# Two gated cross-attention layers on one core: maxima of the first attention read from PSUM, products of ones ahead of TensorE's work, moments by pairs, a new order

## The chip, the cores and the metric

The kernel runs on one core of a Trainium2 chip. A core has a matrix engine (TensorE, PE in the profile, with its weight loads as PEld), three engines for element-wise work (VectorE or DVE, ScalarE or ACT, GpSimd or POOL), and queues that start transfers (here SyncE, SP, and ACT). Each engine works through its own instructions in order and waits for others by semaphores. On-chip memory is SBUF; PE writes its results to PSUM, eight banks of 2 KB in each of 128 partitions, from where DVE or ACT fetch them.

The metric is device time in microseconds, the median of several runs. The profile is one execution, whose span runs from its first to its last instruction.

## The reference

The input `x` has 2 x 1024 rows of 256 features; the context has 2 x 77 rows. Two layers follow each other. Each adds a gated cross-attention (16 heads of 16 features, 77 keys) and a gated feed-forward part. In the first layer the feed-forward part has quantized weights (three levels) and activations (8 bits) and a GELU; in the second it is one expert with a ReLU and a layer norm at its end, since the routing weight is one for expert 0 and zero for the others. The second attention adds a bias from the distances.

```python
x = x + jnp.tanh(g_xattn[0]) * _L0_xattn_ref(_layernorm(x), ctx, ctx_weights...)
x = x + jnp.tanh(g_ffn[0]) * _L0_ffn_ref(_layernorm(x), L0_ffn_w1, L0_ffn_w2)
x = x + jnp.tanh(g_xattn[1]) * _L1_xattn_ref(_layernorm(x), ctx, ctx, distances, ...)
x = x + jnp.tanh(g_ffn[1]) * _L1_ffn_ref(_layernorm(x), ...)
# attention: softmax(q k^T / 4 [- log(distances + 1e-9) * |scaling|]) v, then the output weights
# first FFN: quant(gelu(quant(h) @ quant(w1).T)) @ quant(w2).T
# second FFN: relu(h @ w1 + b1) @ w2 + b2, layer norm of h plus that, times gamma, plus beta
```

All arithmetic is in fp32, apart from the quantized products, whose integers are held in bf16.

## The kernel before

The 2048 rows are 16 tiles of 128 rows, in four groups of four tiles (`GROUPS`). Each group goes through four stages: attention of layer one (`attention(0, g)`), quantized feed-forward (`bit_ffn`), attention of layer two (`attention(1, g)`), expert (`expert_ffn`). Groups don't depend on each other, so stages of different groups overlap.

**Order.** The kernel doesn't issue its work as it is written. Every step (one or a few instructions on one engine) is recorded in a `Plan` with a cost, the tiles that it reads and writes, and for some steps two engines to choose from. `Plan.order` then goes through a list schedule: on each engine the step that can begin first, ties decided by the number that the table `WEIGHTS` (line 52) has for the step. Buffers are given out in the same pass. The steps are issued in the order of their planned begin, and the tile framework adds the semaphores that this order needs. So a step's cost, or its weight, changes where it stands on its engine and which buffer it gets. Transfers are one exception: they are planned in the order in which they are written, and those that ACT starts are issued first of all.

**The beginning.** `fetch` (line 464) starts the transfers: the first group's rows tile by tile on SP, the weights of the first attention on ACT's queue, then the rest. POOL makes constants, one of them `ones` (line 560). PE's first work is `center` (line 765), which takes the mean of the query weights out of them, and the transposes of the first rows (line 663).

**Attention.** For a group, PE transposes the rows (663) and makes the queries (803). Then, for each half of the heads and each pair of tiles, `softmax_pair` runs:

- PE makes the scores of both tiles (827), 16 products into `sc`, four PSUM banks, of which there is one set;
- in the first layer ACT copies each tile's scores to SBUF (the helper's line 427, `probs<-sc`); in the second DVE adds the distance bias on the way (866);
- DVE takes the maximum per row and head from the copy (875), POOL subtracts it (880), ACT takes the exponential (889), DVE sums (897) and takes reciprocals (902), POOL multiplies (906).

`values` then has PE transpose the probabilities (925), ACT copy them (427, `pT<-b`), and PE multiply them by the values (938). The output weights (959) and the gated residual (967) end the stage, with the moments of the new rows.

**Moments.** `stats` (line 587) adds two steps for each tile of 128 rows: `bn_stats` (589) and `bn_aggr` (590). POOL makes the reciprocal root from them (609, 610).

**Feed-forward parts.** `bit_ffn` rounds (1079) and transposes (1093) rows, multiplies by the quantized weights (1132), takes GELU on ACT (1140), takes the maximum of the hidden rows on DVE (1056), rounds, transposes and multiplies again (1156), and adds the residual (1164). `expert_ffn` has two large products, 1192 and 1211. Two tiles share one PSUM bank for the result of 1211; DVE adds it (1227), takes moments (589), and two more steps (1239, 1247) lead to the store. For the last pair of the last group these steps are taken tile by tile.

Of the kernel before, what the change touches and what calls it, by code (L numbers as in the profile page):

```python
# [9 lines left out]
F32 = mybir.dt.float32  # L10
# [6 lines left out]
P = 128  # L17
# [31 lines left out]
LEAVE = 2  # L49

# [3 lines left out]
1245 1326 1308 1686 1626 1573 1612 1393 1342 1295 1643 1706 1629 1687 1420 1685 1486 1673 1711  # L54
1665 1126 1335 1606 1580 433 1173 843 1317 1350 761 989 905 630 1053 674 1167 919 1052 748 1329
710 1713 1547 1634 1720 1705 1597 1557 1717 1684 1455 1518 1562 1497 1633 1664 1651 1649 1417 1691
1504 1642 1698 1690 1696 1718 534 1552 1513 1106 1033 483 1659 1000 1670 718 1407 512 904 491 600
408 699 479 467 1668 1716 1457 1641 1596 1478 1621 1611 1639 1645 1628 1631 1671 1540 1590 1658
1662 1657 1677 1694 1707 1703 1689 1701 1640 1465 1680 1697 1661 1679 1427 1499 1714 1708 1636
1530 1704 1719 1377 1463 1374 1591 1700 1688 1683 1675 1494 1551 1702 1674 1647 1667 1715 1709  # L60
1517 1489 1579 1601 1444 1695 1462 1655 1318 1362 1178 1110 1346 1402 1156 1524 1570 1652 1627
1678 1425 1219 1587 1338 1269 1554 1365 1262 1413 1239 1537 1484 1446 1356 1321 1210 1360 1692
1663 1440 1630 1712 1710 1660 1646 1605 1517 1584 1268 484 885 1297 1035 1699 1625 1672 1608 1682
1693 1592 1621 1635 1410 1560 1530 1345 1488 1514 1614 1411 1526 1449 1404 1432 1649 1525 1533
1603 1472 1604 1599 1624 1576 1543 1516 1581 1560 1582 1366 1452 1399 1506 1615 1588 1281 1403
1653 1632 1472 1654 1456 1487 1249 1522 1527 1572 1236 1306 1438 1290 1666 1624 1173 1272 640 966
1565 271 1166 1072 1567 1151 959 740 1331 1091 1291 1264 1333 1267 1030 916 1182 1138 990 928 1256
983 1012 1120 829 762 1081 961 1235 974 1027 1032 723 677 1034 1499 861 1064 934 883 1261 399 1164
1011 889 1086 1062 1093 893 1154 560 1313 1325 827 1580 584 790 836 738 947 1163 869 1010 1423
1075 1250 1483 786 932 975 1108 845 615 903 1044 633 473 1337 409 1081 1349 840 1043 1401 1372 656  # L70
477 613 924 763 367 324 827 579 750 821 958 665 811 550 606 566 607 524 320 511 297 359 559 362
537 925 833 560 587 463 556 317 745 913 835 1299 1080 891 1016 986 1141 1098 1065 788 1037 777
1327 1104 969 519 1300 912 800 722 705 720 1203 901 799 1289 1253 1085 1111 900 1099 1121 1118 703
852 899 749 505 478 699 775 1041 1005 1090 789 887 908 1134 1185 772 711 724 957 727 315 901 772
796 848 1206 653 993 822 819 690 669 512 670 636 725 1014 975 1132 1102 1130 609 646 644 567 718
756 1201 563 647 948 710 629 627 648 592 1040 808 898 697 582 795 596 500 888 1189 558 520 1336
991 960 1116 856 846 530 818 741 759 976 434 1242 1333 967 1107 915 1055 517 931 576 278 328 319
355 516 394 639 835 558 186 210 241 257 372 295 253 458 684 544 894 444 679 1363 816 1379 1036
1022 1315 920 1419 1109 1538 678 246 759 412 410 358 419 407 366 600 746 726 342 588 594 488 801
216 228 194 312 963 733 487 1026 1183 862 1285 1232 1442 1301 1045 1193 1127 1347 831 1091 912 687  # L80
1424 1528 1529 868 850 512 708 345 752 742 548 635 844 896 851 1257 1135 1149 1171 1110 1051 896
334 341 1271 331 1009 231 301 157 265 343 313 823 855 681 910 369 249 218 266 287 457 510 565 707
619 651 436 154 298 435 572 404 381 153 196 167 161 410 1470 1123 1192 1316 1368 1361 1493 1324
1512 1284 1443 1379 1439 1322 1441 1263 1332 1276 1364 1389 1412 1577 1507 1481 1502 1535 1349
1331 1542 1369 1294 1428 1386 1548 1640 1503 1361 1638 1617 1588 1610 1421 1424 1622 1552 1595
1532 1589 1637 1405 1280 1506 1521 993 1385 1541 1619 1656 1174 1397 1360 1454 1354 1175 1574 1436
1561 1490 1112 1388 1409 1382 1429 1426 1177 1371 1213 1307 826 949 1610 1343 1344 1390 1509 1280
1294 1291 1351 1292 1312 1505 1435 1544 1461 1474 1304 1566 1165 1023 1476 1480 1193 1133 1214
1100 1380 1512 1272 1209 1401 1605 1539 1437 1448 1514 1451 1341 1464 1598 1585 1588 1555 1352
1613 1495 1644 1569 1618 1623 1586 1571 1632 1681 1512 1358 1669 1542 1231 1433 1377 1600 1279  # L90
1357 1536 1534 1607 1620 1568 1048 1278 1314 948 960 1223 1104 678 460 999 874 973 689 955 980
1013 719 822 773 847 1014 1048 1159 1348 367 625 706 474 753 1265 846 655 546 936 858 878 1067 866
555 705 1002 686 764 774 730 613 872 914 780 832 867 506 820 466 323 682 693 915 702 1293 815 1099
768 701 797 770 763 1069 1025 1378 1408 1018 1160 1079 876 950 1339 694 665 346 1063 1387 875 700
691 630 954 789 494 779 661 842 221 422 265 686 414 208 427 193 183 309 264 364 440 368 344 765
585 476 404 537 632 304 644 299 692 535 593 453 438 1508 1247 1447 1520 578 650 1477 1222 1305
1356 1074 1117 326 574 1088 769 380 349 445 397 470 538 574 413 695 582 657 542 557 700 825 496
763 860 623 384 549 879 1113 749 1084 1317 1248 964 917 1221 1185 946 1096 1078 1319 1174 1434 908
1399 951 962 1336 1095 1122 762 995 1283 1479 1468 1249 1147 1398 1000 1434 971 1265 1146 1196
1205 1260 1391 1252 1416 1353 1328 608 787 732 922 1016 942 853 1169 998 1075 1065 1323 1202 732  # L100
1460 1194 386 671 575 622 431 482 501 639 426 388 666 822 399 935 871 672 972 566 238 302 497 305
944 721 918 1144 660 1125 1222 1078 1084 791 247 376 926 739 1243 1517 1212 377 573 729 966 515
743 1021 1266 748 1001 985 714 1038 509 371 895 1162 873 717 751 1482 1054 1212 1286 1101 758 881
754 480 529 307 336 400 470 373 234 262 411 636 1153 1046 784 889 1317 711 782 620 715 325 232 418
624 552 979 1047 690 934 951 803 812 444 766 771 932 966 838 405 884 825 1168 451 878 806 1187
1181 1334 1032 1082 1396 737 1223 1020 1114 1232 713 1208 1140 976 1004 1066 1187 886 1149 1150
540 610 1240 1207 1496 1374 1377 1504 1511 1515 1362 1313 1027 1320 1223 1255 1542 1546 1545 1415
1474 1475 1273 1501 1007 1458 864 870 1075 1145 1296 1105 1228 1218 1217 1211 1192 1156 1259 1191
1087 890 1195 1037 1381 1301 1081 1172 851 1011 1140 1109 793 982 930 1198 1163 1395 1559 1523
1383 1225 1045 1025 1142 1265 1246 1028 1008 997 1077 1137 809 1311 1161 1244 1231 923 929 996 968  # L110
1510 1270 1274 1024 1364 1070 1309 1277 1282 1425 1531 1450 1253 1650 1676 1609 1575 1584 1445
1466 1558 1578 1553 1469 1302 1563 1375 1220 1430 1492 1453 1401 1330 1288 1224 1216 938 1550 1556
1648 1616 1583 1361 1402 1473 1498 1418 1301 1400 1396 1128 1068 1094 988 654 795 554 472 465 1452
779 595 801 849 1062 1066 1205 939 852 1031 1594 1188 1190 1157 1485 1593 1491 1139 747 1148 645
683 401 1029 1179 1061 909 767 350 718 406 1070 673 1067 577 424 643 956 1219 1226 896 694 449
1076 508 811 795 792 1215 911 603 901 810 790 882 329 980 1195 698 1071 692 765 1124 1076 1049 705
1195 1089 561 611 798 931 957 946 953 945 646 958 902 471 518 689 614 230 364 592 545 649 704 375
739 867 443 589 929 786 1166 663 1234 860 1273 834 668 600 709 428 679 972 778 937 1279 1230 1256
1312 1039 1413 696 1306 933 1186 940 992 570 280 318 300 225 786 528 454 490 201 261 308 486 378
365 330 289 316 310 237 486 396 459 539 242 338 139 1177 1282 924 450 197 415 442 127 244 169 314  # L120
269 430 450 449 599 417 779 532 471 755 239 531 177 117 158 120 267 191 254 227 281 500 498 637
568 655 525 675 794 527 1305 598 573 623 856 988 536 449 512 479 676 535 583 920 716 829 465 503
452 514 949 275 332 626 256 590 638 374 245 143 721 1015 187 135 147 390 347 124 121 182 205 160
200 185 229 141 156 163 110 98 62 20 27 91 76 72 151 89 125 162 108 155 150 172 105 142 175 152 17
# [101 lines left out]
class Plan:  # L226
# [45 lines left out]
    def order(self, weight):  # L272
# [13 lines left out]
        while len(done) < len(self.steps):  # L286
            best = None
            for e, waiting in ready.items():
                cand = []
                for s, w, at in waiting:  # L290
# [8 lines left out]
                    for t in s.tiles:  # L299
                        if t in given:  # L300
                            continue
# [1082 lines left out]
```

## Time and profile before

| | |
|---|---|
| median of 3 runs | 372.38 us (371.84 to 373.26) |
| the profiled execution | 373.1 us |
| its span | 371.4 us |
| mean granted clock of TensorE | 0.973 |
| busy: PE, DVE, ACT, POOL | 338.6, 272.3, 238.7, 235.3 us |
| weight loads of PE (beside its products) | 214.7 us |
| subtractions and multiplications on POOL (880, 906) | 128 of 1.25 and 1.27 us |
| maxima and sums on DVE (875, 897) | 128 of 0.78 and 0.77 us |
| copies of scores on ACT (427, `probs<-sc`) | 32 of 0.69 us |

Durations of single instructions include the time in which the engine fills and drains, which overlaps with the next instruction. Where instructions stand back to back, the distance from start to start is the time that one more of them costs: 0.70 us for a maximum, 0.71 for a sum, 1.2 for a step on POOL. In the timeline and the chain, merged rows such as "x2" show this. "Idle before" in brackets names what ended the wait. Busy shares of the whole span mix stages that have different limits; the table by stretches keeps them apart.

### The profile page before, as it was taken

The page shows a single profiled execution, that of the slowest core. Times are in us where ns is not written, and L with a number is a line of the kernel's source. Part 1 is how long each engine was busy: PE and PEld are TensorE (multiplying, and loading weights), DVE is VectorE, ACT ScalarE, POOL GpSimd, SP SyncE. Part 2 cuts the span into 40 slices and gives each one's busy share as a digit, 9 for nine tenths or more (in the row PEclk, how much of TensorE's full clock was granted, in tenths as well). Part 3 has the DMA queues.
Part 4 walks back from the last instruction along what each step waited for, and adds up shares of the span by engine and source line. Part 5 has one row for each costly group of instructions (what it writes and reads, how often), then busy time and mean ns, then how long its engine had stood idle before and what let it go on. Part 6 is the DMA issues. An engine that isn't in the chain of part 4 may idle for free.

```text
span 371.4 us, 5881 instructions
## 1 busy us (share of the span) xinstructions
PE 338.6 (91%) x2148; PEld 214.7 (58%) x2156; DVE 272.3 (73%) x570; ACT 238.7 (64%) x395; POOL 235.3 (63%) x265
## 2 busy tenths in 40 slices
PE   5959899889978989899999999999999999999993
PEld 3535346466554755674474467675488546685582
DVE  3598778899999999999999986397325896074034
ACT  2597879899999897967778472727541386431400
POOL 5399799998995052599989976019213688144012
PEclk9996969998999999999999999999999999999998
DMA  8972002003010000000000000000000100000001
GB/s 236 354 207 41 5 22 92 2 6 109 3 14 3 3 2 0 2 2 2 0 3 0 2 0 2 29 2 0 28 2 22 35 2 1 3 0 29 28 2 57
DMA packets 18150, 12.51 MB, mean 34 GB/s; under 512 B 8647, under 2 KB 17608, under 8 KB 18120
## 3 DMA queue, kind: packets, MB, share of 16 engines
q1 hardware_dynamic: 17300, 11.34, 10.4%
q10 hardware_dynamic: 816, 0.79, 0.6%
q8 instruction: 17, 0.28, 0.3%
q14 instruction: 17, 0.11, 0.1%
HBM read 9.71 MB, written 2.10 MB: 32 GB/s over the span
## 4 chain that ended last, share of the span: by engine, by line
PE 50%; DVE 25%; ACT 10%; POOL 9%; issue 3%; DMA 1%; POOLq 0%; ACTq 0%; DVEq 0%
PE b L1211 14%; PE b L1192 12%; DVE mx L875 5%; POOL probs L880 5%; PE b L925 5%; PE b L938 5%; DVE den L897 4%; DVE probs L866 3%; DVE st L589 3%; PE sc L827 3%; PE b L803 3%; POOL probs L906 3%; DVE x L967 2%; ACT pT L427 2%; DVE top_h L1056 2%
## 5 line engine op out<-in xcount | busy, mean ns | idle before, releaser
L880 POOL TENSOR_TENSOR probs<-probs,mx 128x616 f32<-128x616 f32 x64 | 78.7, 1248 | 14.2 <-DVE mx L875 11.4
L906 POOL TENSOR_TENSOR probs<-probs,den 128x616 f32<-128x616 f32 x64 | 79.7, 1266 | 6.4 <-DVE den L902 4.1
L925 PE MATMUL b<-ident,probs 128*128 128x128 f32 (+1 forms) x320 | 49.4, 286 | 11.8 <-ACT pT L427 4.2
L1211 PE MATMUL b<-staged,hT 128*128 128x256 f32 x256 | 58.6, 381 | 0.6 <-DVE xn L1227 0.6
L1192 PE MATMUL b<-xnT,staged 128*128 128x512 f32 x128 | 57.0, 596 | 0.0
L925 PEld LDWEIGHTS b<-ident,probs 128*128 128x128 f32 (+1 forms) x320 | 36.6, 142 | 31.8 <-POOL probs L906 11.2
L875 DVE TENSOR_REDUCE mx<-probs 128x8 f32<-128x616 f32 x64 | 48.7, 784 | 8.1 <-ACT probs L427 7.3
L897 DVE TENSOR_REDUCE den<-probs 128x8 f32<-128x616 f32 x64 | 48.7, 772 | 7.2 <-ACT probs L889 7.2
L427 ACT ACTIVATE pT<-b 128x512 f32<-128x512 f32 (+1 forms) x80 | 44.4, 601 | 13.6 <-PE b L925 13.4
L1211 PEld LDWEIGHTS b<-staged,hT 128*128 128x128 f32 x256 | 47.5, 190 | 8.4 <-issue 1.5
L609 POOL TENSOR_SCALAR rstd<-mv 128x4 f32<-128x4 f32 (+2 forms) x25 | 7.6, 305 | 65.3 <-DVE mv L590 65.2
L427 ACT ACTIVATE hT<-b,eb_sb 128x512 f32<-128x512 f32 x32 | 21.7, 684 | 27.3 <-PE b L1192 21.5
L1192 PEld LDWEIGHTS b<-xnT,staged 128*128 128x128 f32 x128 | 23.5, 190 | 26.5 <-issue 25.1
L803 PE MATMUL b<-xnT,wq_sb 128*128 128x512 f32 x64 | 35.3, 660 | 0.3 <-ACT xnT L427 0.3
L633 ACT ACTIVATE xn<-x,shift,rstd 128x256 f32<-128x256 f32 x48 | 25.8, 595 | 13.1 <-DVE x L1247 8.5
L938 PE MATMUL b<-pT,vbd 128*32 128x512 f32 (+1 forms) x256 | 33.3, 627 | 0.4 <-ACT pT L427 0.4
L959 PE MATMUL b<-wo_sb,OT 128*128 128x256 f32 x128 | 30.4, 383 | 0.6 <-ACT OT L427 0.5
L589 DVE BATCH_NORM_STATS2 st<-x 128x6 f32<-128x256 f32 x64 | 25.8, 416 | 5.5 <-DMA x<-in_x_dram 4.5
L1227 DVE TENSOR_TENSOR xn<-b,xn 128x512 f32<-128x512 f32 (+1 forms) x9 | 5.7, 632 | 30.8 <-PE b L1211 30.8
L827 PE MATMUL sc<-kbd,qT 32*128 32x154 f32 x512 | 27.6, 325 | 0.6 <-ACT probs L427 0.4
L827 PEld LDWEIGHTS sc<-kbd,qT 32*128 32x128 f32 x512 | 19.4, 189 | 14.0 <-issue 3.4
L959 PEld LDWEIGHTS b<-wo_sb,OT 128*128 128x128 f32 x128 | 23.5, 190 | 5.5 <-ACT OT L427 1.2
(102 smaller groups left out, 541.1 us busy)
## 6 DMA issues: line engine op xcount, KB each, us to landing
staged<-in_ew_dram SPq DMA_DIRECT2D x2, 1024.0 KB
out_dram<-x SPq DMA_DIRECT2D x7, 256.0 KB
x<-in_x_dram SPq DMA_DIRECT2D x6, 256.0 KB
staged<-in_fw1T_dram SPq DMA_DIRECT2D x1, 1024.0 KB
staged<-in_fw2T_dram SPq DMA_DIRECT2D x1, 1024.0 KB
dbias<-in_dist_dram SPq DMA_DIRECT2D x1, 616.0 KB
x<-in_x_dram SPq DMA_DIRECT2D x4, 128.0 KB
wo_sb<-in_woT_dram SPq DMA_DIRECT2D x2, 256.0 KB
```

The costliest lines, as they stand in the source:

```text
L427: nc.scalar.activation(out(), src(), AF.Relu if relu else AF.Copy if bias is None else AF.Identity, bias=0.0 if bias is None else bias(), ...
L803: lambda h=h, k=k, pq=pq: nc.tensor.matmul(pq.ap, wq_sb.ap[:, k, h * P : (h + 1) * P], xnT.ap[:, k, :], start=(k == 0), stop=(k == KT - 1),),
L827: nc.tensor.matmul(sc.ap[:, q, j * QK : j * QK + QK], qT.ap[rows, h, at : at + P], kbd.ap[rows, h, b].rearrange("p h s -> p (h s)"), start ...
L875: lambda j, n: nc.vector.tensor_reduce(each(mx, j, n), heads(j, n), AX.X, ALU.max),
L880: lambda e, j, n: e.tensor_tensor(heads(j, n), heads(j, n), bc(each(mx, j, n), 2, SK), ALU.subtract),
L897: lambda j, n: nc.vector.tensor_reduce(each(den, j, n), heads(j, n), AX.X, ALU.add),
L906: lambda e, j, n: e.tensor_tensor(heads(j, n), heads(j, n), bc(each(den, j, n), 2, SK), ALU.mult),
L925: lambda j=j, c=c, m=m, tr=tr: nc.tensor.transpose(tr.ap[:m, j, :], prs[j // 2].ap[:, j % 2, c * P : c * P + m], ident.ap),
L938: nc.tensor.matmul(po.ap[32 * q : 32 * q + 32, :], vbd.ap[: CH[c], b, h, s, :], pTs[c].ap[: CH[c], :], start=(i < 4), stop=(i >= 4),)
L959: nc.tensor.matmul(pp.ap[:, j % 2, :], OT.ap[:, k, j * P : (j + 1) * P], wo_sb.ap[:, k, :], start=(k == 0), stop=(k == KT - 1),)
L1192: lambda f=f, k=k, ph=ph: nc.tensor.matmul(ph.ap, ew1_sb.ap[:, k, f * P : (f + 1) * P], xnT.ap[:, k, :], start=(k == 0), stop=(k == KT - 1),),
L1211: lambda j=j, f=f, pp=pp: nc.tensor.matmul(pp.ap[:, j % 2, :], hT[f].ap[:, j * P : (j + 1) * P], ew2_sb.ap[:, f, :], start=(f == 0), stop= ...
```

## The change

Five things change.

1. In the first layer the maximum (875) reads the scores in PSUM instead of the copy in SBUF. The copy stays, and the subtraction still needs both. The reduction keeps its order of elements in both layers.
2. `WARM` = 14 products of `ones` by `ones` into an unused PSUM tile are the first step of PE. `ones` is now made first.
3. `stats` takes one or two tiles in one step: both `bn_stats`, then both `bn_aggr`. Pairs are used after attention, after the expert, and for the rows of the later groups; single tiles for the first group's rows, after `bit_ffn` and for the last pair.
4. The last pair of the last group gets a PSUM bank for each tile.
5. The planner has new costs (transfers, copies, maxima, residuals, moments), keeps a step from beginning before the buffer of its tile is free, and has a new table of weights. The order on every engine is new. The first group's rows and weights are written in another sequence, which changes their place in the plan and not on their queues.

The number of instructions is almost the same: PE has 14 products more, ACT loads its tables eleven times instead of nine, one addition of a bias goes from DVE to POOL. In the new order the first layer's third group comes ahead of its second, and the expert of the first group begins ahead of the second attention of the second group, which it followed before.

```diff
+WARM = 14
 WEIGHTS = tuple(
...
                     for t in s.tiles:
                         if t in given:
+                            begin = max(begin, born[t])
                             continue
...
-                given[t] = min(slots[key])[1]
+                born[t], given[t] = min(slots[key])
...
-    def fetch(eng, t, src, cols=None):
+    def fetch(eng, t, src, cols=None, cost=None):
...
-            max(0.47, size / 0.28),
+            cost or max(0.47, size / 0.3),
...
+    fetch_x0(0, 1.6)
+    wq0_sb = fetched_w(nc.scalar, "wq0_sb", wqT0, None, 0.6)
+    fetch_x0(1, 0.5)
+    fetch_x0(2, 1.1)
+    wk0_sb = fetched_w(nc.scalar, "wk0_sb", wkT0, None, 0.6)
+    fetch_x0(3, 0.7)
...
+    warm = lazy(ps_b, [P, P], F32, "b", 4)
+
+    def warm_up():
+        for _ in range(WARM):
+            nc.tensor.matmul(warm.ap, ones.ap, ones.ap, start=True, stop=True)
+
+    pe(0.23 * WARM, warm_up, [ones], [warm])
...
-    def stats(src, mv, j):
-        st = lazy(sm, [P, 6], F32, "st", 4)
-        dve(0.39, lambda: nc.vector.bn_stats(st.ap, src.ap), [src], [st])
-        dve(0.09, lambda: nc.vector.bn_aggr(mv.ap[:, j, :], st.ap), [st], [(mv, j)])
+    def stats(mv, srcs):
+        st = {j: lazy(sm, [P, 6], F32, "st", 4, own) for own in [Set(len(srcs))] for j in srcs}
+
+        def fn():
+            for j, src in srcs.items():
+                nc.vector.bn_stats(st[j].ap, src.ap)
+            for j in srcs:
+                nc.vector.bn_aggr(mv.ap[:, j, :], st[j].ap)
+
+        n = len(srcs)
+        dve(
+            0.05 + 0.45 * n if n > 1 else 0.55, fn, list(srcs.values()),
+            list(st.values()) + [(mv, j) for j in srcs],
+        )
...
-                        (c_act(n * HK), c_dve(n * HK)), lambda: f(0), lambda: f(1), r, w
+                        (0.58 * n, c_dve(n * HK)), lambda: f(0), lambda: f(1), r, w
...
-                1, lambda f, r, w, n: dve(0.07 + n * 0.65, f, r, w),
-                lambda j, n: nc.vector.tensor_reduce(each(mx, j, n), heads(j, n), AX.X, ALU.max),
-                [pr], [mx],
+                1, lambda f, r, w, n: dve(0.74 if layer == 0 else 0.71, f, r, w),
+                lambda j, n: nc.vector.tensor_reduce(
+                    mx.ap[:, j].rearrange("p (q h) -> p q h", q=4),
+                    (
+                        sc.ap[:, :, j * QK : j * QK + QK] if layer == 0 else
+                        pr.ap[:, j].rearrange("p (q f) -> p q f", q=4)
+                    ).rearrange("p q (h s) -> p q h s", s=SK),
+                    AX.X, ALU.max,
+                ),
+                [sc] if layer == 0 else [pr], [mx],
...
-            pp = bank("pp", (P, 2, D))
+            last = g == len(GROUPS) - 1 and i == n // 2 - 1
+            pp = [bank("pp", (P, 2, D)) for _ in range(1 + last)]
...
-                            pp.ap[:, j % 2, :], hT[f].ap[:, j * P : (j + 1) * P],
+                            pp[-(j % 2)].ap[:, j % 2, :], hT[f].ap[:, j * P : (j + 1) * P],
```

## The prediction

> **What bounds the kernel now.** I read three views of the profile: busy time of each engine in stretches, the chain that ended last, then the timeline around the places the change touches. The stretches first; columns are busy us (instructions) of PE, weight load, DVE, ACT, POOL, then the granted clock, DMA share and GB/s.
>
> ```profile
> 16.00:60.00 44.00, 36.44 (x253) 20.73 (x252) 36.87 (x80) 37.46 (x60) 40.77 (x37) 0.84 0.35 97
> 60.00:100.00 40.00, 35.87 (x299) 22.62 (x301) 37.31 (x77) 36.19 (x63) 37.90 (x37) 0.96 0.08 27
> 100.00:156.00 56.00, 49.59 (x399) 31.72 (x392) 53.29 (x117) 51.25 (x81) 29.38 (x43) 1.00 0.04 4
> 156.00:200.00 44.00, 41.54 (x331) 24.99 (x330) 42.65 (x87) 34.37 (x64) 40.51 (x41) 1.00 0.00 1
> 200.00:365.00 165.00, 162.92 (x828) 106.90 (x830) 94.64 (x198) 74.41 (x123) 78.55 (x84) 1.00 0.03 10
> ```
>
> Three regimes follow each other. Up to 100 us POOL is fullest (40.8 of 44, 37.9 of 40): it subtracts maxima and multiplies by reciprocals. From 100 to 200 DVE is (53.3 of 56, 42.7 of 44). After 200 PE is full at full clock and nothing else matters until its last product. So an edit early on pays only if it lets DVE or POOL deliver earlier, or leaves PE less to do after them.
>
> The chain: start, us, what.
>
> ```profile
> 0.78 3.51 DMA wq_sb<-in_wqT_dram
> 4.43 2.04 PE b L765 x4
> 6.48 1.82 PE b L663 x8
> 8.30 1.91 PE b L803 x2
> 12.24 1.72 PE b L803 x4
> 13.96 0.78 PE sc L827 x16
> 14.76 1.27 ACT probs L427 x2
> 16.05 0.81 DVE mx L875
> 16.93 6.76 POOL probs L880 x6
> 182.01 1.42 DVE den L897 x2
> 362.77 2.87 PE b L1211 x12
> ```
>
> PE starts slow: two records of L803 take 1.91 us at 8.30, four take 1.72 at 12.24, so it ran at half pace from 4.43 to about 10.3. The first maximum starts only when both copies are out (14.76 + 1.27). From the timeline:
>
> ```profile
> 38.73 1.50 DVE L875 TENSOR_REDUCE mx<-probs 128x8 f32<-128x616 f32 x2 [2.88 <-ACT probs L427]
> 155.85 0.75 DVE L1079 TENSOR_SCALAR hs<-hs,up_h 128x1024 f32<-128x1024 f32 x1
> 362.77 2.86 PE L1211 MATMUL b<-staged,hT 128*128 128x256 f32 x12 [0.59 <-DVE xn L1227]
> ```
>
> The first is a DVE stall behind a late PE, the third a PE stall at the very end. The second is the handoff that I sum along: the last rounding of the second group's hidden rows. Before it DVE has 131.4 us of instructions since the first maximum, counted at their distances where they stand back to back, in a stretch of 156.6 - 16.05 = 140.55: 9.2 us idle. After it PE has 197.4 us of products counted the same way, in 365.6 - 156.6 = 209.0: 11.6 us lost. The last product is 5.8 us before the end of the span.
>
> **The change part by part.** The profiled execution took 373.1 us, its span 371.4 and 1.7 around it; the median of the runs is 372.4, 0.7 lower. The sum is a difference that I take off both.
>
> Products of ones. They wait for one memset, which ends at 0.98 in this trace and stays first, so PE starts near 1.1 instead of 4.43. They stand ahead of everything on PE's queue. Cold, 128 columns cost about 1.91 / 4 = 0.48, warm 1.72 / 8 = 0.22; fourteen are 6.7 us cold or 3.1 warm. The slow spells later in the trace last 6.8, 6.8 and 3.4 us, so I take the clock to open 3.4 to 6.8 us after work begins (5.9 here). Opening at 4.5, the products end at 6.0; opening at 7.9, they end at 7.8, still cold. Before, the first scores start 9.46 us after PE does, 5.9 of them at half pace, so 6.5 us of full-speed work lies ahead of them. That gives scores at 12.5 to 14.4 against 13.89. I take 13.2: 0.7 gained, ends 1.4 gained and 0.5 lost.
>
> The Trainium skill, TensorE: Matmul & The Clock Gate, Part 1, says that warm-up is some 3.4 us of sustained work against a free-running window, not a number of products; by it fourteen cold products are more than is needed and hold back real work that could warm the array as well. By its 3.4 us the scores would start at 12.5, which would make the sum 0.7 lower; the trace shows 5.9.
>
> Maxima from PSUM. 32 of 64 reductions read the scores. Nearest rows: the same reduction from SBUF at 0.70 (den: 0.71) and the bias add reading the same scores (L866, mean 0.78 against 0.78 for L875): extra cost 0, end +2.2 (32 x 0.07); no gain, since as many elements are read. The gain should be the copy's time. But in the built program the copies on ACT and the maxima on DVE of one pair wait for each other: in six of sixteen pairs strictly copy, maximum, copy, maximum, in the others in two or three turns, never both at once. So the first maximum waits for one copy instead of two: scores 13.2, copy begins 0.87 later, lasts 0.63 and hands over 0.1, maximum at 14.8 instead of 16.05: -1.25 with the products' 0.7 in it. In exchange the second maximum waits on ACT, and ACT's second copy on DVE, with the exponentials of other tiles queued behind it. Six times 0.7 is 4.2 us of DVE waiting, none of it real where DVE was idle anyway (9.2 us in this stretch); ends 0 and 4.2, I take 2.1.
>
> The Trainium skill, PSUM — Partial Sum Buffer, PSUM bank collisions raise a hardware error, says that no two engines may read one bank and quadrant at once. By it the overlap can't be had at all; with a true overlap the first maximum would start 0.7 earlier still. No run here shows a collision.
>
> Order. In the stretch from the first maximum to the corresponding rounding (now the second group's second tile) DVE gets, against before: 4 maxima at 0.70, 7 sums at 0.71, 8 reciprocals at 0.12, 4 bias adds at 0.71, 4 residual adds at 0.76 (+14.6); 3 FFN residuals at 0.49, 4 hidden roundings at 0.75, 3 absolute maxima at 1.2, 3 scales at 0.31 fewer (-9.0); input side of the FFN +3.4; moments +2.0 (38 sets, mostly in pairs at 0.97, against 33 single ones at 0.52). Together +11.0. PE has less left: 6 and 6 products of L1192 and L959 at 0.87, 48 transposes at 0.115, 2 of L938's sets at 1.86, 4 of scores at 0.37 fewer (-21.2), FFN products and transposes more (6 x 0.43 + 4 x 0.87 + 1.8 = +7.9): -13.3. Net -2.3. Pairing moments is inside this: 1.09 us for two sets one by one (358.70 to 359.79) against 0.97, and POOL's reciprocal roots wait 0.4 longer for the first of a pair; free, since POOL had waited 65 us at that line.
>
> Stalls. PE stood idle 22.9 to 26.2 because POOL did six subtractions (16.93 on) before its first multiplication; then came a spell of half clock to 34.2, and DVE's 2.88 us at 38.73 follow from late scores. Now POOL's first multiplication comes after three subtractions and one reciprocal root (3 x 1.2 + 1.27 against 7.1), and projections of two later groups fill PE. I take this stall away: -2.9; ends 0 and all 9.2 of DVE's idle time. What is late next is POOL itself, 93% full there.
>
> Last pair in two banks. L1227 of the third tile no longer holds the fourth tile's products: -0.6, all on the path, since only its own sum, moments and store follow; the other end is 0, should the clock or the weights of those products set their pace. DMA: same queues, same transfers; the costs edited are the planner's. The second expert weight is fetched after the second layer's scattered values; its first use is over 80 us later. ACT loads two more tables (1.28 each) in stretches where it idles 14.4 of 100 us: +0.5, ends 0 and 2.6.
>
> Sum: -1.25 + 2.1 - 2.3 - 2.9 - 0.6 + 0.5 = -4.45. The profiled 373.1 becomes 368.6, the median 372.4 becomes **368.0 us**.
>
> **Rivals.** *The scores' bank becomes the bound (slower).* Scores can be overwritten after both copies, 1.26 us, before; now after copy, maximum, copy, maximum with four handoffs, 0.63 + 0.70 + 0.63 + 0.70 + 0.4 = 3.1. With 0.74 of products and a handoff a pair takes 4.0 us; POOL needs 4 x 1.21 = 4.84 per pair. If DVE, 84% to 93% full there, reaches the maxima later than 0.8 us on average, POOL starves. At 1.3 us late: 16 x 0.5 = 8 us more, 376. It decides against the change beyond about 1.1 us. For it: only one set of score banks. Against: POOL's margin.
> *Nothing gained (same).* The stall stays or comes back elsewhere (-2.9 gone), the waits cost 4.2 instead of 2.1: 372.4 - 4.45 + 5.0 = 373.0. For it: the clock spells hang on idle gaps that an order moves but doesn't remove.
> *More gained.* DVE's idle time falls by 8 instead of 2.9, since expert products now fill PE during the FFN: 363. Against: POOL stays full to 100 us.
>
> **How the numbers follow.** Forecast 0.43 (366 to 370.4), more gained 0.21, nothing gained 0.17, bank the bound 0.19. The range runs from 361.5 to 376: it leaves out a few in 100 below and the far half of the slower case. About 0.5% (1.9 us) is what a measurement of this kernel tells from no change: faster 0.64, same 0.17, slower 0.19.
>
> **What would show it.** Right: scores near 13.2, the first maximum near 14.8 with ACT's second copy after it; no half clock near 27 to 34; DVE idle before the rounding at 6 to 8 us; the last L1211 run without a break; POOL over 90% to 100 us. Wrong: POOL waiting for maxima, score products waiting for DVE, or a half-clock spell as long as before.

## The result and the profile after

The changed kernel is slower. Its median is 376.97 us (376.25 to 377.55, 4 runs) against 372.11 us (370.29 to 373.26, 4 runs) for the kernel before beside it: a ratio of 1.0136, 95% interval 1.0101 to 1.0171. The forecast was 368.0. The profiled execution took 376.25 us, with a span of 374.5; before it was 373.1 and 371.4. So the medians differ by 4.9 us and the two profiles by 3.1: the profiled execution of the changed kernel is its fastest, the one before lies above its median. What is read from the profiles accounts for these 3.1 us.

The same stretches as before; columns are us, then busy us (instructions) of PE, weight load, DVE, ACT and POOL, then the granted clock, DMA share and GB/s.

```profile
16.00:60.00 44.00, 33.13 (x254) 19.06 (x248) 34.51 (x71) 35.12 (x55) 38.35 (x37) 0.96 0.41 105
60.00:100.00 40.00, 32.65 (x245) 19.30 (x246) 34.31 (x78) 36.52 (x62) 34.85 (x36) 1.00 0.09 28
100.00:156.00 56.00, 50.53 (x423) 32.21 (x426) 52.48 (x108) 49.74 (x83) 45.61 (x45) 0.97 0.01 2
156.00:200.00 44.00, 41.30 (x255) 24.52 (x260) 35.12 (x82) 35.53 (x57) 14.89 (x25) 1.00 0.00 1
200.00:365.00 165.00, 163.85 (x932) 107.37 (x927) 104.86 (x211) 81.19 (x136) 93.77 (x95) 1.00 0.03 10
```

Up to 100 us POOL and DVE are busy for less of the time than before: POOL 38.4 and 34.9 instead of 40.8 and 37.9, DVE 34.5 and 34.3 instead of 36.9 and 37.3. That is so although the granted clock is better (0.96 instead of 0.84 in the first row). The fullest engine between 60 and 100 us is now ACT, with 36.5 of 40; POOL and DVE wait more than before. After 200 PE is full as before, a little more so.

The chain that ended last: start, us, what.

```profile
3.21 6.32 PE b L572 x28
31.92 1.27 ACT probs L424 x2
62.07 1.38 DVE mx L900 x2
85.53 1.27 ACT probs L424 x2
142.42 1.49 DVE mx L900 x2
355.02 13.66 PE b L1243 x62
```

The products of ones (line 572) are now the first long piece of the path. Copies of scores (the helper's line 424) and maxima (900) follow each other along it, where one was meant to run beside the other. The last 62 records of 1243 run without the break of 0.59 us that the kernel before had.

The timeline of the changed kernel at the front, at the handoff used for the sum, and at the end:

```profile
3.21 6.32 PE L572 MATMUL b<-ones 128*128 128x128 f32 x28 [3.21 <-POOL ones L552]
15.70 0.81 PE L851 MATMUL sc<-kbd,qT 32*128 32x154 f32 x16
16.57 0.68 ACT L424 ACTIVATE probs<-sc 128x616 f32<-128x616 f32 x1 [0.17 <-PE sc L851]
17.29 0.80 DVE L900 TENSOR_REDUCE mx<-sc 128x8 f32<-128x616 f32 x1 [2.57 <-ACT probs L424]
18.12 0.68 ACT L424 ACTIVATE probs<-sc 128x616 f32<-128x616 f32 x1 [0.87 <-DVE mx L900]
18.84 0.80 DVE L900 TENSOR_REDUCE mx<-sc 128x8 f32<-128x616 f32 x1 [0.75 <-ACT probs L424]
19.69 0.81 PE L851 MATMUL sc<-kbd,qT 32*128 32x154 f32 x16 [1.27 <-DVE mx L900]
174.69 1.40 DVE L1110 TENSOR_SCALAR hs<-hs,up_h 128x1024 f32<-128x1024 f32 x2
355.02 13.65 PE L1243 MATMUL b<-staged,hT 128*128 128x256 f32 x62 [0.35 <-ACT hT L424]
```

Lines two to seven are one pair of tiles: scores, copy, maximum, copy, maximum, and only then the next scores, each waiting for the one ahead of it as its bracket says. In the whole trace none of the 32 copies runs at the same time as a maximum of scores. The first line contradicts the prediction and also a sentence of the section on the change, "`ones` is now made first". It is written first in the code, but the planner lays the fill eighth on POOL; it runs at 2.95 us (0.78 in the kernel before), and the products wait for it until 3.21.

The time can be cut at three points, as in the prediction: the start of the first maximum, the end of the corresponding rounding (155.85 + 0.75 before; now 174.69 + 0.74, the first of the two in that row), and the end of the span. DVE's busy time in the second part is the union of its instructions; the prediction counted some 3 us more, since it took instructions at their distances.

| us, from the profiles | before | changed | difference |
|---|---|---|---|
| first maximum starts | 16.05 | 17.29 | +1.24 |
| from there to the rounding: DVE busy | 128.08 | 139.59 | +11.5 |
| from there to the rounding: DVE idle | 12.48 | 18.55 | +6.1 |
| from the rounding to the end | 214.8 | 199.1 | -15.7 |
| span | 371.4 | 374.5 | +3.1 |

So DVE takes over 11.5 us of work ahead of the handoff, what follows shrinks by 15.7, and this is eaten up by 6.1 us of new idle time and a later start.

### The profile page after: what moved, and what is told of

It is laid out like the page before. It is cut to its first block, busy times and chain, and to the rows that moved or that the text cites. A ratio compares the mean times of both kernels' runs of the same rounds, so it can differ in the third digit from the quotient of the medians.

```text
span 374.5 us, 5929 instructions
## 1 busy us (share of the span) xinstructions
PE 337.9 (90%) x2175; PEld 216.2 (58%) x2184; DVE 271.6 (73%) x569; ACT 242.0 (65%) x397; POOL 237.0 (63%) x266
## 3 DMA queue, kind: packets, MB, share of 16 engines
q1 hardware_dynamic: 17300, 11.34, 10.5%
## 4 chain that ended last, share of the span: by engine, by line
PE 50%; DVE 20%; ACT 17%; POOL 8%; issue 3%; POOLq 0%; ACTq 0%; DVEq 0%
PE b L1243 15%; PE b L1223 13%; DVE mx L900 5%; DVE den L929 4%; PE b L957 4%; ACT probs L424 4%; ACT pT L424 3%; PE sc L851 3%; PE b L970 3%; DVE st L606 3%; ACT xn L657 3%; PE b L991 3%; ACT hs L1171 2%; PE b L827 2%; POOL probs L938 2%
## 5 line engine op out<-in xcount | busy, mean ns | idle before, releaser
L912 POOL TENSOR_TENSOR probs<-probs,mx 128x616 f32<-128x616 f32 x64 | 77.5, 1227 | 28.3 <-DVE mx L900 24.7
L1243 PE MATMUL b<-staged,hT 128*128 128x256 f32 x256 | 60.6, 382 | 0.3 <-ACT hT L424 0.3
L1223 PE MATMUL b<-xnT,staged 128*128 128x512 f32 x128 | 58.5, 596 | 0.3 <-ACT xnT L424 0.3
L424 ACT ACTIVATE pT<-b 128x512 f32<-128x512 f32 (+1 forms) x80 | 43.5, 604 | 15.4 <-PE b L957 14.9
L991 PE MATMUL b<-wo_sb,OT 128*128 128x256 f32 x128 | 31.4, 385 | 3.3 <-DVE x L999 1.7
L827 PE MATMUL b<-xnT,wq_sb 128*128 128x512 f32 x64 | 32.8, 627 | 1.7 <-ACT xnT L424 1.7
L890 DVE TENSOR_TENSOR probs<-sc,dbias 128x616 f32<-128x616 f32 x32 | 24.7, 782 | 9.8 <-PE sc L851 9.8
L900 DVE TENSOR_REDUCE mx<-sc 128x8 f32<-128x616 f32 x32 | 24.7, 785 | 9.8 <-ACT probs L424 9.2
L921 ACT ACTIVATE probs<-probs 128x616 f32<-128x616 f32 x32 | 22.3, 719 | 10.6 <-POOL probs L912 10.5
L606 DVE BATCH_NORM_STATS2 st<-x 128x6 f32<-128x256 f32 x64 | 24.8, 417 | 5.9 <-DMA x<-in_x_dram 4.9
```

The lines of the kernel that those rows point to most:

```text
L424: nc.scalar.activation(out(), src(), AF.Relu if relu else AF.Copy if bias is None else AF.Identity, bias=0.0 if bias is None else bias(), ...
L827: lambda h=h, k=k, pq=pq: nc.tensor.matmul(pq.ap, wq_sb.ap[:, k, h * P : (h + 1) * P], xnT.ap[:, k, :], start=(k == 0), stop=(k == KT - 1),),
L900: lambda j, n: nc.vector.tensor_reduce(mx.ap[:, j].rearrange("p (q h) -> p q h", q=4), (sc.ap[:, :, j * QK : j * QK + QK] if layer == 0 el ...
L912: lambda e, j, n: e.tensor_tensor(heads(j, n), heads(j, n), bc(each(mx, j, n), 2, SK), ALU.subtract),
L991: nc.tensor.matmul(pp.ap[:, j % 2, :], OT.ap[:, k, j * P : (j + 1) * P], wo_sb.ap[:, k, :], start=(k == 0), stop=(k == KT - 1),)
L1223: lambda f=f, k=k, ph=ph: nc.tensor.matmul(ph.ap, ew1_sb.ap[:, k, f * P : (f + 1) * P], xnT.ap[:, k, :], start=(k == 0), stop=(k == KT - 1),),
```

## The experiments

Three theories stood against each other. The *serial reads*: copy and maximum wait for each other, and the new order was planned as if they did not. The *late products*: they push the front back. The *order*: it is worse on this chip, whatever the reads. Ratios below are to the kernel before, run beside each; its medians in these sets are 372.1 to 373.1 us, so differences between medians of different sets are good to about 1 us.

**The products taken out.**

```diff
-        for _ in range(WARM):
+        for _ in range(0):
```

> The changed kernel without its 14 products of ones (they add nothing to the output), all else in its order. Theory of the late products: in the changed kernel they hold TensorE from 3.21 to 9.53 us, and the first score product starts at 15.70 instead of 13.89; without them the scores start at 13.7 to 14.3, the first maximum at 15.3 to 15.9 (from 17.29), and the time falls by 1 to 2 us to 375 to 376. Theory of the serial reads (copy and maximum of the same scores wait for one another) and theory of the order (its steps are laid worse for this chip, whatever the reads): the front is filled up again by later waits, and the time moves by less than 0.5 us.

Measured: 376.52 us (376.13 to 376.99), ratio 1.0086 (1.0052 to 1.0121), against 1.0136 (1.0101 to 1.0171) with the products; the intervals overlap, and the medians differ by 0.45. The scores start at 14.71, later than the theory said. PE's first transposes now wait for rows by DMA, until 6.60 us for the third one, so that dropping the late products brings the front only 1.0 us forward, and the part up to the rounding took 1.6 longer in this profile, with half clock for 13.7 us instead of 6.8. Late products are little worse than none. This does not say yet what early ones are worth.

**The fill first.**

```diff
     ones = const("ones", [P, P], F32, lambda t: nc.gpsimd.memset(t, 1.0), 0.2)
+    plan.steps[-1].first = True
```

> The changed kernel with the fill of ones as GpSimd's first instruction instead of its eighth. Theory of the late products: the products then start near 1.1 us (fill seen at 0.78 in the kernel before) instead of 3.21, the granted clock opens near 7.2 instead of 9.38, the scores start near 13.6 instead of 15.70, the first maximum at 15.2 instead of 17.29, and the time falls by 1 to 2 us. The other two theories: the front moves alike, but the time by less than 0.5 us.

Measured: 374.02 us (373.19 to 375.94), ratio 1.0055 (1.0024 to 1.0086), 2.95 below the changed kernel's median. The timeline of this kernel:

```profile
1.04 6.34 PE L573 MATMUL b<-ones 128*128 128x128 f32 x28 [1.04 <-POOL ones L552]
13.54 0.81 PE L852 MATMUL sc<-kbd,qT 32*128 32x154 f32 x16
15.13 0.80 DVE L901 TENSOR_REDUCE mx<-sc 128x8 f32<-128x616 f32 x1 [0.45 <-ACT probs L424]
```

Everything at the front stands 2.16 us earlier than in the changed kernel, and nothing behind it has moved: 158.14 us from the first maximum to the rounding in both, 199.06 and 199.07 from there to the end. The theory of the late products holds, at 2.2 us between the profiles, a little more than the 1 to 2 expected. But with it mended the kernel is still slower than before.

**The maxima from the copy again, in the changed order.** The diff leaves out a helper that keeps each maximum behind its copy in the order issued.

```diff
-                    (
-                        sc.ap[:, :, j * QK : j * QK + QK] if layer == 0 else
-                        pr.ap[:, j].rearrange("p (q f) -> p q f", q=4)
-                    ).rearrange("p q (h s) -> p q h s", s=SK),
+                    pr.ap[:, j].rearrange("p (q f) -> p q f", q=4).rearrange(
+                        "p q (h s) -> p q h s", s=SK
+                    ),
```

> The changed kernel with the first attention's maxima taken from the copy in SBUF again, each kept behind its copy, all other steps in the changed order. Theory of the serial reads: VectorE's idle time between the first maximum and the rounding of the second group's last hidden row falls from 15 to 16 us to 9 to 11, GpSimd's wait for maxima (24.7 us in 13) to 11 to 14, and the time by 4 to 6 us to 371 to 373. Theory of the order: the idle time stays above 14, and the time moves by less than 1 us. Theory of the late products: no change to within 0.5 us, the scores still start at 15.7.

Measured: 377.53 us (377.06 to 377.85), ratio 1.0114 (1.0083 to 1.0145): no better than the changed kernel. The waits of this kernel: who waits for what, us in total, times, longest.

```profile
POOL probs L940 <- DVE mx L927: 28.3, 18, 6.0
DVE mx L927 <- ACT probs L451: 13.9, 10, 3.0
PEld sc L878 <- DVE mx L927: 0.9, 2, 0.8
```

The bank is released early again (the next scores wait 0.9 us for maxima), and yet DVE waits longer for copies, 13.9 us instead of 9.2, and is idle for 20.8 us up to the rounding instead of 18.6. My expectation was wrong: a maximum that reads the copy stands behind it just as one that waits its turn at the bank. The place of the read alone is not the cause. What both have in common is that the order was laid out for a maximum beside its copy. The kernel's own planner shows this: in the plan of the changed order 19 of the 32 maxima begin before the copy of the same scores ends, in the plan of the kernel before none does. By the numbers set ahead, this run went as the theory of the order said (idle above 14 us, less than 1 us of change). The next pair tells whether that order is bad in itself or bad because of the waits.

**The maxima free of every wait, in both orders.** The true maxima are left out; a reduction of the same size reads the keys, which lie in SBUF.

```diff
-                        sc.ap[:, :, j * QK : j * QK + QK] if layer == 0 else
-                        pr.ap[:, j].rearrange("p (q f) -> p q f", q=4)
-                    ).rearrange("p q (h s) -> p q h s", s=SK),
+                    bc(kbd.ap[:, h, b], 1, 4) if layer == 0 else
+                    pr.ap[:, j].rearrange("p (q h s) -> p q h s", q=4, s=SK),
```

> The changed kernel with the first attention's 32 maxima taken from the block-diagonal keys, which lie in SBUF long before, over the same 8 x 77 elements: the true maxima are left out, and with them every wait between a maximum, its copy and the next scores. All else in the changed order. It bounds from above what any freeing of these reads can give. Theory of the serial reads (the changed order is good, the waits between copy and maximum spoil it): VectorE's idle time between the first maximum and the rounding of the second group's last hidden row falls from 15 to 16 us to below 10, GpSimd's wait for maxima from 24.7 us to below 12, and the time by 4 to 6 us to 371 to 373. Theory of the order: less than 2 us, and the idle time is put down to other releasers instead.

> The kernel before with the same: the first attention's maxima taken from the keys, the true maxima left out, its order kept. Here maxima wait for copies only (7.3 us in 5 spells), and GpSimd waits for maxima for 11.4. Theory of the serial reads: much less is to be had than in the changed kernel, 0 to 2 us (370.5 to 372.5). Theory of the order: as much as in the changed kernel or more, so that the old order stays ahead of the new by 3 us or more with free maxima too.

Measured: in the changed order 368.52 us (366.52 to 369.32), ratio 0.9901 (0.9861 to 0.994), 8.45 below the changed kernel. In the old order 370.69 us (369.85 to 372.35), ratio 0.9967 (0.9945 to 0.999), 1.6 below the kernel before. The waits that involve maxima, in the changed kernel and then in the one with free maxima:

```profile
POOL probs L912 <- DVE mx L900: 24.7, 13, 6.0
DVE mx L900 <- ACT probs L424: 9.2, 10, 2.6
ACT probs L424 <- DVE mx L900: 6.3, 9, 1.3
PEld sc L851 <- DVE mx L900: 5.4, 6, 2.1
```

```profile
POOL probs L910 <- DVE mx L900: 16.7, 10, 6.0
PEld sc L851 <- DVE mx L900: 0.9, 2, 0.8
```

Two of four rows are gone. DVE waited for copies (9.2 us) and ACT's copies for maxima (6.3); neither does any more. DVE's idle time up to the rounding falls from 18.6 to 13.1 and that part from 158.1 to 152.0 us, with the same instructions on every engine. The expectation had idle time below 10 us and POOL's wait below 12 (16.7 measured), and yet the time fell by more than the 4 to 6 us it gave. The spans differ by 8.3 us: 6.1 in that part, 2.1 ahead of it, where the first maximum now follows a reduction of weights and no longer waits for its copy. Some of this is chance: the clock opened at 6.33 us here and at 9.38 in the changed kernel's profile, so the scores start 1.5 us earlier. So the waits cost between 6.8 and 8.3 us in these profiles, and 8.45 is the difference of the medians. As these maxima do not even wait for the scores, this is the most that freeing the reads could give in this order. The theory of the order falls: without these waits the new order is ahead of the old one, 0.9901 against 0.9967.

**The maxima from PSUM in the old order.** The part done alone, with the next scores kept behind the maxima.

```diff
-                lambda j, n: nc.vector.tensor_reduce(each(mx, j, n), heads(j, n), AX.X, ALU.max),
+                lambda j, n: nc.vector.tensor_reduce(
+                    mx.ap[:, j].rearrange("p (q h) -> p q h", q=4),
+                    (
+                        sc.ap[:, :, j * QK : j * QK + QK] if layer == 0 else
...
```

> The kernel before with one part of the change: the first attention's maxima read from PSUM, so that a copy and a maximum of the same scores, and the next scores, wait for one another; its order otherwise kept. Theory of the serial reads: slower by 4 to 8 us (376 to 380), with VectorE's idle time before the 32 maxima at 7.3 us or more from copies and GpSimd's wait for maxima above 20 us (11.4 before). Theories of the order and of the late products: within 1 us of the kernel before, in either direction.

Measured: 378.93 us (378.01 to 380.59), ratio 1.0161 (1.0125 to 1.0197), 6.4 above the kernel before. The waits of this kernel:

```profile
POOL probs L916 <- DVE mx L902: 18.6, 13, 4.6
DVE mx L902 <- ACT probs L454: 12.4, 12, 2.0
PE sc L854 <- DVE mx L902: 7.3, 6, 1.9
PEld sc L854 <- DVE mx L902: 5.6, 5, 2.0
```

In the kernel before POOL waits 11.4 us for maxima, DVE's maxima 7.3 for copies, and PE's weight loads for scores 1.0. Here the bank is held longer as well, so PE waits too. (POOL's 18.6 us stay below the 20 expected.) This part does not pay in either order: in the old one it costs 6.4 us, in the new one it makes no clear difference (376.97 against 377.53 with the copy). Neither the order nor the place of the read is the cause alone. With maxima from the copy, from PSUM and free, the old order takes 372.3, 378.9 and 370.7 us, the new one 377.5, 377.0 and 368.5.

**The small parts, in the old order.** Products of ones in front of everything, then the last pair in two banks, then both.

```diff
+    def prelude():
+        ones_step.fn()
...
+        for _ in range(WARM):
+            nc.tensor.matmul(bank, ones.ap, ones.ap, start=True, stop=True)
```

> The kernel before with the fill of ones and 14 products of ones in front of everything on GpSimd and TensorE. Theory of the late products: the products run from near 1.1 to about 4.4 us, where the transposes start in the kernel before (4.43), the granted clock opens near 7.3 instead of 10.32, the scores start at 12.7 to 13.3 instead of 13.89, and the time falls by 0.7 (0 to 1.4) us. Rival, after the run without products, where a first maximum 1.0 us earlier gave 0.5 us: less than 0.5 us.

```diff
-            pp = bank("pp", (P, 2, D))
+            last = g == len(GROUPS) - 1 and i == n // 2 - 1
+            pp = [bank("pp", (P, 2, D)) for _ in range(1 + last)]
```

> The kernel before with the last pair's products in two banks of PSUM instead of halves of one. Prediction's term: minus 0.6 us, the wait of the last products for the first half's sum gone. Rival: the wait was covered, less than 0.3 us.

> The kernel before with its own order and the two small parts together: the fill of ones and 14 products in front of everything, and the last pair in two banks. From the single runs, minus 0.7 and minus 0.9 against 372.3: 370.4 to 371.2 if they add up; 371.2 to 372 if an earlier start is swallowed by later waits.

Measured: the products alone 371.52 us (369.93 to 373.37), ratio 0.9978 (0.995 to 1.0005); the banks alone 371.38 us (370.35 to 374.38), ratio 0.9987 (0.9956 to 1.0017); both 370.62 us (369.93 to 372.57), ratio 0.9962 (0.9934 to 0.9989). Each alone is not resolved from no change, both together are. With the products alone the scores start at 13.04 us, as expected, although the products end at 6.04 and not near 4.4. The banks are clear in the profiles. From the rounding to the end the span takes 214.8 us in the four old-order kernels without them and 214.0 in the two with them, 0.8 less. In the timeline of the kernel with two banks alone the last products run through:

```profile
351.74 11.39 PE L1212 MATMUL b<-staged,hT 128*128 128x256 f32 x52
```

**The moments one by one, in the changed order.**

```diff
             for j, src in srcs.items():
                 nc.vector.bn_stats(st[j].ap, src.ap)
-            for j in srcs:
                 nc.vector.bn_aggr(mv.ap[:, j, :], st[j].ap)
```

> The changed kernel with each tile's two moment instructions one after the other inside the same step, instead of both of the first kind and then both of the second. By the prediction's term, 1.09 us for two tiles against 0.97, the 18 pairs ahead of the second group's last rounding cost VectorE up to 2.2 us more, of which its idle time hides a part: 0 to 2 us slower than the changed kernel (377 to 379). Rival: pairing gains nothing, within 0.5 us of 377.

Measured: 378.14 us (377.61 to 380.8), ratio 1.0158 (1.0114 to 1.0202). DVE's busy time up to the rounding rises from 139.6 to 141.8, by 2.2 us. That this is the number worked out ahead (18 pairs, 0.97 against 1.09) is luck: from its start to the next instruction a pair takes 0.89 us in the changed kernel, not 0.97, against 1.09 here, and there are 16 pairs in that part, not 18, which makes 3.2 us; 1.1 of it lies in short gaps behind the moment instructions, which are not busy time. The time is 1.2 above the changed kernel's, though the two intervals overlap. Pairing is a small gain on DVE.

**An order that knows the wait.** The maxima read the copy, the plan is told that they depend on it, the fill is first, and the table of weights is new: random changes of it were kept when the plan's end came earlier. In this plan no maximum begins before the copy of the same scores ends. Nothing is left out of the computation.

```diff
+    plan.steps[-1].first = True
...
-                        sc.ap[:, :, j * QK : j * QK + QK] if layer == 0 else
...
-                [sc] if layer == 0 else [pr], [mx],
+                [pr], [mx],
```

> The changed kernel with its maxima taken from the copy, the planner told so (each maximum depends on its copy in the plan), the fill of ones first, and a new table of weights that was searched for this plan. Nothing of the computation is left out. Theory of the serial reads: the changed order lost because it was planned with copy and maximum at once; an order that knows the wait keeps what the kernel with free maxima showed, and comes to 368 to 370 us, with VectorE waiting for copies for less than 7 us ahead of the maxima. Theory of the order (a table searched in this planner's model does not carry over to the chip, with or without the reads): 372 us or more.

Measured: 367.93 us (367.67 to 368.58), ratio 0.9875 (0.9834 to 0.9915). It is the fastest here and beats both kernels. Its waits on maxima and copies:

```profile
POOL probs L912 <- DVE mx L901: 28.7, 13, 10.5
DVE mx L901 <- ACT probs L424: 3.8, 2, 2.2
PEld sc L852 <- DVE mx L901: 0.8, 1, 0.8
```

DVE waits for copies twice, for 3.8 us. Cut at the same points, with the eighth rounding in order as in the changed kernel (here the last of the third group): the first maximum at 15.02, then 131.6 us of DVE work and 11.0 idle, then 208.6 to the end. Against the kernel before that is -1.0, +3.5, -1.5 and -6.2. It moves work to the other side of the handoff as the changed kernel does, only less of it, and buys no idle time with it. The first row warns against reading one wait as a measure: POOL waits longer for maxima here, 28.7 us, than in the slow kernel, because one wait of 10.5 ends at 274 us, where PE is full and nothing hangs on POOL. One step is not separated: how much of this gain a newly searched table would have brought without the other changes.

A layout in which the copy of one half runs beside the maximum of the other would need the halves in different banks. It was not tried, because two of the four products that run side by side on different rows of PE's array (16 records of 0.32 us on average pass in 0.81) would then write to one bank. The Trainium skill, PSUM — Partial Sum Buffer, section PSUM bank collisions raise a hardware error, leaves it to software to keep such writes apart; no run here shows them.

## Why the prediction was wrong, point by point

The prediction's terms, put together by the same cuts:

| us | predicted | profiles |
|---|---|---|
| first maximum | -1.25 | +1.24 |
| DVE's work up to the rounding | +11.0 | +11.5 |
| DVE's idle time there (waits +2.1, stall -2.9, tables +0.5) | -0.3 | +6.1 |
| from the rounding on (PE's products -13.3, two banks -0.6) | -13.9 | -15.7 |
| sum | -4.45 | +3.1 |

*Waits between copy and maximum, +2.1: the step that failed most.* I counted only the six pairs that are strictly serial, one wait of 0.7 us each, and halved the sum because DVE had idle time to hide it. With the maxima free the part up to the rounding falls by 6.1 us and the median by 8.45. The kernel before had such waits too: with free maxima it gains 1.2 us in that part and 1.6 by the median. So the waits that the change added cost 4.9 us of that part, 6.9 by the medians, where 2.1 was predicted. Ten copies made DVE wait, nine maxima made ACT wait, and the planner, with 19 of 32 maxima set beside or ahead of their copy, had put other work behind both as if neither happened. Each late maximum is a late subtraction, exponential and sum.

*Stall, -2.9: did not come.* The half-clock spells shrank as expected, from 17.1 to 6.8 us (without the one at the end), and the stall of 2.88 us at 38.73 went with them. But POOL's first multiplication starts at 24.01, where it started at 23.97 before, no earlier, and other waits took the stall's place: one sum alone waits 3.28 us for an exponential:

```profile
52.55 0.80 DVE L929 TENSOR_REDUCE den<-probs 128x8 f32<-128x616 f32 x1 [3.28 <-ACT probs L921]
```

Even with the maxima free DVE is idle for 13.1 us up to the rounding, 0.6 more than before: 6.7 of that is sums waiting for exponentials, 2.4 before. So less half clock (10.2 us of it in that profile, 17.1 before) did not bring DVE's idle time down; what the exponentials in turn wait for was not taken apart.

*Products, and the first maximum: the mechanism was right, the place wrong.* "One memset ... stays first" was taken from the code and not from the instruction stream. With the fill first the products start at 1.04, the scores at 13.54 (13.2 predicted) and the maximum 1.59 behind them (1.6 predicted). The gain of 0.7 us for early products was met in the old order, 0.74 between medians, though not resolved alone.

*Order, -2.3:* right in direction. DVE's work was off by 0.5 us, and the part after the rounding shrank by 1.8 more than predicted. Inside DVE's work the moments, +2.0, were summed too high: at the distances in the traces 33 sets before take 16.1 us and 38 now 17.5, which is +1.4. The counting of instructions on both sides of a handoff held; what stood between them, idle time, did not.

*Two banks, -0.6:* 0.8 in the profiles. *Pairs of moments:* 2.2 us of DVE's busy time by experiment. *Table loads, +0.5:* not measured by themselves; they sit in the idle row.

*Extra cost of reading PSUM, 0:* right. A maximum took 785 ns from PSUM and 784 from SBUF in the kernel before.

*Rivals.* "The scores' bank becomes the bound", 376 us, came closest: its sign and size were right, and so was POOL waiting for maxima (11.4 to 24.7 us) and score products waiting for DVE (5.4 us), both named as signs of a wrong forecast. Its mechanism was only half right. The run with maxima from the copy set the bank free and gained nothing; it is the maximum behind the copy that is late, with or without the bank.

The program never read the scores' banks with two engines at a time, as said of the trace above; the prediction expected this from the waits of the built program and then priced them too low. The Trainium skill, PSUM — Partial Sum Buffer, section PSUM bank collisions raise a hardware error, says that no two engines may read one bank and quadrant at once. The trace agrees, and no run here shows a collision.

## What to carry to other kernels

Moving a read to an earlier copy of the data gains nothing if the two readers must take turns there, and a planner that believes in the overlap builds an order that pays for it many times over: check each pair that a plan puts side by side against the waits of the built program. Price a new wait by what is queued behind it on both engines, not by its own length times its count. And where an instruction stands on its engine is read from the instruction stream, never from its place in the source.

## What the runs showed of the hardware

The clock opened between 3.1 and 6.2 us after the products of ones began, with nothing ahead of them on PE. They began at 3.20 or 3.21 us in four profiles, where it opened at 6.33 (free maxima), 8.10, 9.20 and 9.38 (changed kernel); they began at 1.04 in four others, where it opened at 4.31, 4.44, 5.45 and 7.24. The half-clock spells inside the kernels last 3.41 or 6.83 us in every profile. Both fit windows of 3.41 us that run on without regard to the kernel. No window has to be busy from end to end for the clock to open: with free maxima it opened 3.13 us after the first product, PE's first work, which is less than one window. The products' own length shows the spread: 6.32 us in the changed kernel, 4.87 with free maxima. So one profile's front can differ from the next by some 1.5 us for this reason alone (the scores above), and single fronts of one kernel should not be compared closer than that unless the clock opened at the same distance, as it did in the changed kernel (6.17) and with the fill first (6.20).

The Trainium skill, TensorE: Matmul & The Clock Gate, Part 1, gives a free-running window of 3.4 us and says that the transition varies by half a microsecond either way; the windows agree with these runs, the spread of 3.1 us does not.
